# The first expert block's products with down_embed as stages of each group's mlp during the scan, kept in DRAM

## Chip, cores and metric

One core of a Trainium2 chip runs the whole kernel as one program. The metric is the device time of one execution in microseconds; less is better.

## What is computed

x has 4 x 1024 tokens of width 256, all in f32. Four layers follow one another, each added to x after a layer norm (ln):

```python
x = x + attn_a(ln(x))   # state-space block: projections, a convolution of 4 taps, a scan with 16 states per channel
x = x + ffn(ln(x))      # first expert block
x = x + attn_b(ln(x))   # linear attention, 16 heads
x = x + ffn(ln(x))      # second expert block
```

The change is in the first `ffn`. With h = ln(x), per token:

```python
queries = (h @ W_q).reshape(2, n, 64); routing = einsum('tnd,tdk->tnk', queries, keys)
# the 8 best of each half, and the 8 best of their 64 sums, choose the experts and give `scores`
ew = silu(einsum('nh,nkh->nk', h, down_embed[indices])) * softmax(scores)
experts = einsum('nk,nkh->nh', ew, up_embed[indices])
mlp = (silu(h @ gate_w) * (h @ up_w)) @ down_w
ffn = mlp + experts
```

There are 512 experts. The kernel doesn't gather their rows: it multiplies h with all 512 rows of down_embed, takes silu, and multiplies with a table that is zero but for the chosen experts.

## The kernel before, in words

The 4096 tokens are worked on in 8 groups of 512 (`G`); two groups are one sequence of the batch. A tile with features on the 128 partitions and a group's 512 tokens along the row is 128x512; 512 experts are four such pieces (`XC`), the mlp's 1024 inner channels eight (`IC`).

**The scan.** `ssm` (line 142) runs 8 groups x 16 states = 128 steps, each in two half steps (`half`, 256 in all). A half step has, on ACT, two decays `a` (`decay`, 908); on POOL, one product `u` (`times_b`, 889), made three half steps ahead; on DVE, two scans `h<-a,u`; then, for the step before (`sum_up`, 919), eight transposes `hT` on PE and two accumulations `acc` on DVE. In this text half steps are numbered from 0 to 255, so that group g begins with half step 32 g.

**What runs beside the scan.** After the scan's own instructions of a half step, `tick` (681) adds stages of other work. A stage is the code between two `yield`s of a generator, and the `yield` states its cost on PE and on ACT. There are three queues: `prep` (`prepare`, 333: the next group's projections, convolution and step sizes), `ends` (`finish`, 495, and `norm`, 544: the end of the group before, its layer norm and the transposed `hT`, stored to the DRAM tensor `hs`) and `mlps` (`mlp`, 574). `tick` takes stages as far as budgets allow, 3.2 us of PE time and 2.7 of ACT time a half step. Everything here is recorded through `Pinned` (37), so each engine runs these instructions in the order in which the code emits them, and all of them carry line 47 in the profile.

**The mlp of a group** has 8 gate stages (two matmuls, 128x512, and one stage later ACT's copy into `av`), one silu over `av`, 8 up stages, and 8 down stages (two for each of 4 token tiles). A product with up is multiplied into `av` either by ACT's copy (`up_v`) and POOL, or by DVE from PSUM; `room` decides (580). Each token tile of the down product is added to x by DVE (`xw<-xw,down`). The weights are streamed in pieces of 128 KB through three buffers (`ask_w`, 534), 8 of gate_w, then 8 of up_w, for each group. At the end x is stored to the DRAM tensor `xs`, and `load_x(g + 4)` (640) asks for the tile of x that reuses its buffer.

At the 27th half step of group g (line 978) the sums over x of group g + 2 begin:

```python
if q % (2 * N) >= 26 and g + 2 < NG and g + 2 not in counted:
    while g + 2 not in xw:
        mlps.stage()
    counted.add(g + 2)
    stats = statistics(g + 2)
```

`statistics` (241) begins with four ACT instructions (`junk<-xw`) that read that tile of x.

**The block.** `experts` (1505) follows the scan. For each group it runs 8 steps. `route` (1309) finds the best experts on DVE and builds the table `tb` on ACT (`entries`) and POOL. `apply` (1553) makes four products `emb` of `hT` with down_embed (two matmuls each), four silus into `wt`, multiplies `wt` by the transposed table (`st` on PE, `weigh` on DVE), and makes the products `o` with up_embed, which DVE adds to x. `hT` is loaded from `hs`. `beside` (1631) takes further stages from `ends` and `mlps`, by a table `COST` of each step's own PE time, until both are empty; then, from group 4 on, `attention_pools` loads the attention's weights, and `attend` runs stages of `first_batch` (1057), the layer norms, keys and queries of the first sequence. At the start of a group's steps, the code first runs all stages that its x still needs (`while g not in rest.stored`).

`attention` (1125) and `ffn` (1734) come last and aren't touched.

Of the kernel before, what the change touches and what calls it, by code (L numbers as in the profile page):

```python
# [12 lines left out]
F32 = mybir.dt.float32  # L13
I16, BF16 = mybir.dt.int16, mybir.dt.bfloat16
AF = mybir.ActivationFunctionType
# [5 lines left out]
P = 128  # L21
B, L, D = 4, 1024, 256
NT = B * L
KD = D // P
G = 512
NG = NT // G
# [25 lines left out]
class Net:  # L52
# [86 lines left out]
        return ps  # L139


    def ssm(self, xs, hs, behind):


        nc, tc, io = self.nc, self.tc, self.io
# [3 lines left out]
        with ExitStack() as ctx:  # L149
# [18 lines left out]

            xw, gates, norms, bcds, sums, first = {}, {}, {}, {}, {}, {}
            ended, gated_all, stored = {-2, -1}, {-2, -1}, set()  # L170

            def load_x(g):
                xw[g] = late4.tile([P, TG, D], F32, tag="x", name="xw")
# [356 lines left out]
                ended.add(g)  # L530

            ahead_w, asked_w = [], [0]

            def ask_w():
                i = asked_w[0]
                if i < NG * 2 * IC:
                    name = "gate_w" if i // IC % 2 == 0 else "up_w"
                    w = late3.tile([P, KD, P], F32, tag="gu", name=name)
                    src = io[name].rearrange("(k p) (c m) -> c p k m", p=P, m=P)
                    sp.dma_start(out=w, in_=src[i % IC])  # L540
                    ahead_w.append(w)
                    asked_w[0] += 1

# [30 lines left out]
            def mlp(g, hT):  # L574
# [437 lines left out]
            for half in range(2):  # L1012
# [2 lines left out]
            scan.close()  # L1015
            behind(
                SimpleNamespace(
                    engines=engines, ends=ends, mlps=mlps, bank=bank, stored=stored,
                    route0=route0, first_h=first_h, key_w=key_w, lates=lates,
                )  # L1020
            )
# [480 lines left out]
                self.x[g][:, t, :], self.x[g][:, t, :], ps, ALU.add  # L1502
            )

    def experts(self, w, xpool, xs, hs, rest):


        tc, nc, ends, mlps, bank = self.tc, rest.engines, rest.ends, rest.mlps, rest.bank
        with ExitStack() as ctx:
# [16 lines left out]
            asks, hT, routes, tables = dict(rest.first_h), {}, {}, {}  # L1526
            self.x, self.total = {}, {}

            half = NG // 2

            def load(into, g):
                while g == NG - 1 and ends.next_cost():
                    ends.stage()
                tag = "hT" if into is hT else f"ask{g // half}"
                into[g] = two.tile([P, KD, G], F32, tag=tag, name=tag)
                nc.sync.dma_start(out=into[g], in_=hs[g])

            def product(ps, pairs):
                for i, (lhsT, rhs) in enumerate(pairs):
# [12 lines left out]

            def apply(g):

                h = hT.pop(g)
                wt = two.tile([P, XC, G], F32, tag="wt", name="wt")

                def emb(c):
                    ps = bank([P, G], "emb")
                    cs = slice(c * P, (c + 1) * P)  # L1560
                    product(ps, [(w["down_embT"][:, k, cs], h[:, k, :]) for k in range(KD)])
                    return ps
# [7 lines left out]
                yield  # L1570
                ps = emb(1)
                yield
                silu(1, ps)
                yield
                yield
                for c in (2, 3):
                    if c == 3:
                        silu(2, ps)
                    ps = emb(c)
                    yield  # L1580
                silu(3, ps)
# [74 lines left out]
            next(routes[0])  # L1656
            next(routes[0])
            beside(1.7)
            load(hT, 0)
            applied = []  # L1660
            for step in range(8 * NG + 7):
                g, k = step // 8, step % 8
                if k == 0 and g < NG:
                    while g not in rest.stored:
                        ends.stage()
                        mlps.stage()
                    self.x[g] = xpool.tile([P, TG, D], F32, tag=f"x{g}", name=f"x{g}")
                    self.total[g] = xpool.tile([P, TG], F32, tag=f"sum{g}", name=f"sum{g}")
                    nc.sync.dma_start(out=self.x[g], in_=xs[g])
                if k == 1 and g < NG:  # L1670
                    applied.append(apply(g))
                for a in list(applied):
                    if next(a, self) is self:
# [3 lines left out]
                if g + 1 < NG:  # L1677
# [3 lines left out]
                        next(routes[g + 1])  # L1681

                    if k == 5 and g % 2 == 0 and g + 2 < NG:
                        load(asks, (g + 2) // 2)
                        load(asks, (g + 2) // 2 + half)
# [80 lines left out]
def build(nc, io, out):  # L1766
    with tile.TileContext(nc) as tc, ExitStack() as ctx:
        net = Net(ctx, tc, io)
        kept = ctx.enter_context(tc.tile_pool(name="kept", bufs=1, space=DRAM))
        xs = [kept.tile([P, TG, D], F32, tag=f"xs{g}", name=f"xs{g}") for g in range(NG)]  # L1770
        hs = [kept.tile([P, KD, G], F32, tag=f"hs{g}", name=f"hs{g}") for g in range(NG)]
        w = net.expert_weights(ctx.enter_context(tc.tile_pool(name="ex_w", bufs=1)))

        def behind(rest):
            xpool = ctx.enter_context(tc.tile_pool(name="x", bufs=1, reuse_waits="tile"))
            net.experts(w, xpool, xs, hs, rest)

        net.at_ctx = ExitStack()
        net.ssm(xs, hs, behind)
# [55 lines left out]
```

## Time and profile before

| | us |
|---|---|
| median of 3 runs (1937.09 to 1939.22) | 1938.54 |
| the profiled execution | 1938.45 |
| its span, first to last instruction | 1936.7 |
| PE busy, of the span | 1767.3 (91%) |
| DVE busy | 1487.1 (77%) |
| ACT busy | 1178.7 (61%) |
| POOL busy | 996.9 (51%) |
| last scan of DVE ends at | 1033.4 |
| 32 products `emb` (128 matmul records) | 60.6 |
| 32 silus `wt<-emb` | 19.0 |

PE is TensorE's matmuls, PEld its weight loads, DVE VectorE, ACT ScalarE, POOL GpSimd, SP the engine that issues most DMAs. One f32 matmul of the program is two records in the profile. Times in the views are microseconds from the span's start, unless marked ns. A row of the timeline has start, time taken, engine, line, operation, output and inputs by the program's names, shapes, count, and in brackets the idle time before it and what ended it. The profile's share for an engine is an average over the scan (to 1033 us), the block (to some 1295 us) and the two last layers.

### The profile page before, as it was taken

What the parts mean: (1) busy time and instruction counts of PE and PEld (TensorE: products, weight loads), DVE (VectorE), ACT (ScalarE), POOL (GpSimd) and SP (SyncE); (2) the same over time, 40 slices, a digit from 0 to 9 for tenths busy, and PEclk for the clock granted to TensorE, in tenths of its full rate; (3) what the DMA queues carried; (4) which work ended last, traced back from release to release, by engine and by line L of the source; (5) the groups of instructions that cost most, each with busy time, mean ns of one, the idle gap of its engine ahead of it and who ended that gap; (6) DMA issues with size and microseconds to landing.
All of it is one profiled execution on the core that took longest, in us unless ns stands there. A gap on an engine that the chain in (4) does not pass through costs nothing.

```text
span 1936.7 us, 22863 instructions
## 1 busy us (share of the span) xinstructions
PE 1767.3 (91%) x7450; PEld 1138.9 (59%) x7450; DVE 1487.1 (77%) x2653; ACT 1178.7 (61%) x2335; POOL 996.9 (51%) x810
## 2 busy tenths in 40 slices
PE   7867789989889898898978999899999999999999
PEld 4445446556456465565645757566666566655665
DVE  6999999999999999999999979734549544433441
ACT  5876798787987878878555664744434333323330
POOL 4978989899988988888862122221111000000000
PEclk8868899999999999999999999999999999999999
DMA  4212121221322212212133121120000000000000
GB/s 127 65 34 60 40 88 54 82 72 57 94 64 73 79 47 82 79 47 77 50 101 127 61 63 68 61 65 1 1 1 1 11 11 12 0 12 11 11 12 11
DMA packets 79928, 97.48 MB, mean 50 GB/s; under 512 B 7360, under 2 KB 53312, under 8 KB 79808
## 3 DMA queue, kind: packets, MB, share of 16 engines
q1 hardware_dynamic: 74592, 90.66, 14.8%
q10 hardware_dynamic: 5216, 5.36, 0.9%
q8 instruction: 59, 0.97, 0.2%
q14 instruction: 61, 0.50, 0.1%
HBM read 83.15 MB, written 12.85 MB: 50 GB/s over the span
## 4 chain that ended last, share of the span: by engine, by line
PE 40%; DVE 9%; ACT 4%; issue 1%; POOL 0%; DVEq 0%; ACTq 0%; POOLq 0%
PE ps L136 23%; PE o L47 3%; PE emb L47 2%; PE down L47 2%; PE at L47 1%; PE up L47 1%; DVE acc L47 1%; PE gate L47 1%; DVE kept L1392 1%; PE st L1470 1%; DVE h L47 1%; PE tr L127 1%; PE route L1304 1%; PE hT L47 1%; ACT a L47 1%
## 5 line engine op out<-in xcount | busy, mean ns | idle before, releaser
L47 POOL TENSOR_TENSOR u<-dx,bt 128x1024 f32<-128x1024 f32 x255 | 601.9, 2363 | 79.6 <-DVE h L47 66.0
L47 DVE TENSOR_TENSOR_SCAN h<-a,u 128x512 f32<-128x512 f32 x512 | 608.1, 1226 | 16.5 <-ACT a L47 14.2
L47 PE MATMUL hT<-ident,h 128*128 128x128 f32 x2048 | 310.8, 292 | 104.0 <-DVE acc L47 103.7
L47 ACT ACTIVATE a<-delta,a_neg 128x512 f32<-128x512 f32 x512 | 340.1, 688 | 96.8 <-DVE h L47 96.0
L47 PEld LDWEIGHTS hT<-ident,h 128*128 128x128 f32 x2048 | 246.1, 149 | 240.9 <-DVE acc L47 195.8
L47 DVE SCALAR_TENSOR_TENSOR acc<-hT,cT,acc 128x512 f32<-128x512 f32 x512 | 353.9, 731 | 12.4 <-PE hT L47 11.4
L1460 POOL TENSOR_TENSOR tb<-tb,kept 128x1024 f32<-128x1024 f32 x16 | 34.0, 2130 | 364.7 <-DVE kept L1453 364.7
L1731 DVE TENSOR_TENSOR act<-s,ps 128x512 f32<-128x512 f32 x64 | 43.9, 686 | 146.3 <-PE ps L136 145.5
L47 PE MATMUL up<-hT,up_w 128*128 128x512 f32 x256 | 131.2, 637 | 11.0 <-ACT up_v L47 10.8
L1729 ACT ACTIVATE s<-ps 128x512 f32<-128x512 f32 x64 | 38.2, 597 | 168.4 <-PE ps L136 168.3
L47 PE MATMUL gate<-hT,gate_w 128*128 128x512 f32 x256 | 122.1, 600 | 0.0
L136 PE MATMUL ps<-hT,w_gate_w 128*128 128x512 f32 x256 | 120.6, 592 | 0.0
L136 PE MATMUL ps<-hT,w_up_w 128*128 128x512 f32 x256 | 120.5, 592 | 0.0
L136 PE MATMUL ps<-w_down_w,act 128*128 128x256 f32 x512 | 117.5, 380 | 1.9 <-DVE x L1501 1.9
L47 POOL TENSOR_TENSOR xc<-xc,tap 128x512 f32<-128x512 f32 x84 | 109.1, 1299 | 18.8 <-ACT tap L47 18.6
L47 PE MATMUL down<-w_down_w,av 128*128 128x256 f32 x512 | 118.1, 379 | 0.0
L136 PEld LDWEIGHTS ps<-w_down_w,act 128*128 128x128 f32 x512 | 95.7, 190 | 20.3 <-DVE x L1501 7.7
L47 ACT ACT_TABLE_LOAD x77 | 98.8, 1283 | 13.8 <-DMA w_wd2T<-in_wd2T 8.9
L47 PEld LDWEIGHTS down<-w_down_w,av 128*128 128x128 f32 x512 | 94.9, 190 | 16.7 <-issue 5.5
L47 POOL TENSOR_TENSOR tb<-tb,kept 128x1024 f32<-128x1024 f32 x16 | 34.8, 2175 | 126.3 <-DVE kept L47 44.3
L1384 ACT ACTIVATE tb<-d,ex 128x64 f32<-128x64 f32 x256 | 62.1, 334 | 45.0 <-DVE ex L1375 42.0
L47 PEld LDWEIGHTS up<-hT,up_w 128*128 128x128 f32 x256 | 47.8, 202 | 61.3 <-issue 40.4
(301 smaller groups left out, 3089.3 us busy)
## 6 DMA issues: line engine op xcount, KB each, us to landing
bt<-bcd SPq DMA_DIRECT2D x127, 256.0 KB, 3.3
gate_w<-in_gate_w SPq DMA_DIRECT2D x64, 128.0 KB, 2.3
up_w<-in_up_w SPq DMA_DIRECT2D x64, 128.0 KB, 2.3
in_wT<-in_in_wT SPq DMA_DIRECT2D x8, 512.0 KB, 4.8
hs<-hT SPq DMA_DIRECT2D x8, 512.0 KB, 2.9
xs<-xw SPq DMA_DIRECT2D x8, 512.0 KB, 2.7
hT<-hs SPq DMA_DIRECT2D x8, 512.0 KB, 5.2
x<-xs SPq DMA_DIRECT2D x8, 512.0 KB, 4.6
```

The costliest lines, as they stand in the source:

```text
L47: return self.tc.keep_in_program_order(f(*args, **kw))
L127: self.nc.tensor.transpose(ps[:, t * P : (t + 1) * P], src[:, t, k * P : (k + 1) * P], self.ident)
L136: self.nc.tensor.matmul(ps, lhsT=lhsT, rhs=rhs, start=i == 0, stop=i == len(pairs) - 1)
L1304: nc.tensor.matmul(ps[:, t, m, :], lhsT=h[:, k, col], rhs=w["scores"][t][:, k, :], start=k == 0, stop=k == KD - 1,)
L1384: nc.scalar.activation(tbv[:, m, i, :], d[:, M4 + m, 0:NKEY], AF.Copy, scale=ex[:, m, i : i + 1],)
L1392: dve.tensor_tensor(kept, v[:, M4:, :].unsqueeze(3).to_broadcast(shk), r[:, M4:, :].unsqueeze(2).to_broadcast(shk), ALU.is_gt,)
L1460: nc.gpsimd.tensor_tensor(tbv[:, ms], tbv[:, ms], kept[:, ms], ALU.mult)
L1470: self.nc.tensor.transpose(st[:, c, :], tb[:, i, c * P : (c + 1) * P], self.ident)
L1729: nc.scalar.activation(s, pg, AF.Silu)
L1731: nc.vector.tensor_tensor(a, s, pu, ALU.mult)
```

## The change

The four products of h with down_embed leave `apply` and become four stages of `mlp`, between the gate stages and the silu. Their weights are streamed as 4 further pieces of 128 KB a group. Each product is copied by ACT to an SBUF tile (`emb_v`, of the same two buffers as `up_v`) and stored to a new DRAM tensor `es[g]`. In the block, `load_wt` loads the 128x2048 tile of a group from `es`, and `apply` begins with one silu over it. `hT` is no longer loaded there. `apply` starts six steps later than before, so that its steps after the silu stand where they stood; the loads of x move by as much. `COST` and the budget of `beside` are changed (3.3 a step instead of 3.5).

```diff
+            shelved = set()
...
             ahead_w, asked_w = [], [0]
+            stream = [
+                (name, c)
+                for name, n in (("gate_w", IC), ("down_embT", XC), ("up_w", IC))
+                for c in range(n)
+            ]
...
-                if i < NG * 2 * IC:
-                    name = "gate_w" if i // IC % 2 == 0 else "up_w"
+                if i < NG * len(stream):
+                    name, c = stream[i % len(stream)]
...
-                    sp.dma_start(out=w, in_=src[i % IC])
+                    sp.dma_start(out=w, in_=src[c])
...
                 act.copy(av[:, IC - 1, :], ps)
+
+                def shelve(c, ps):
+                    t = late2.tile([P, G], F32, tag="up", name="emb_v")
+                    act.copy(t, ps)
+                    sp.dma_start(out=es[g][:, c, :], in_=t)
+
+                for c in range(XC):
+                    yield 1.7, (0.6 if c else 0)
+                    if c:
+                        shelve(c - 1, ps)
+                    ps = bank([P, G], "emb")
+                    w = ahead_w.pop(0)
+                    mul(ps, [(w[:, k, :], hT[:, k, :]) for k in range(KD)])
+                    ask_w()
+                yield 0, 0.6
+                shelve(XC - 1, ps)
+                shelved.add(g)
                 yield 0, 6.4
                 act.activation(av, av, AF.Silu)
...
+            def load_wt(g):
+                while g not in rest.shelved:
+                    ends.stage()
+                    mlps.stage()
+                wts[g] = two.tile([P, XC, G], F32, tag="wt", name="wt")
+                nc.sync.dma_start(out=wts[g], in_=es[g])
...
             def apply(g):
 
-                h = hT.pop(g)
-                wt = two.tile([P, XC, G], F32, tag="wt", name="wt")
-
-                def emb(c):
...
-                def silu(c, ps):
-                    nc.scalar.activation(wt[:, c, :], ps, AF.Silu)
-
-                ps = emb(0)
+                wt = wts.pop(g)
+                nc.scalar.activation(wt, wt, AF.Silu)
                 yield
-                silu(0, ps)
...
-            COST = (0.9, 1.7, 0.9, 1.7, 3.4, 4.3, 1.7, 1.7)
+            COST = (0.9, 0, 0.9, 0, 3.4, 5.1, 0, 0)
 
             def beside(cost):
-                left[0] = min(left[0] + 3.5, 6.0) - cost
+                left[0] = min(left[0] + 3.3, 6.0) - cost
...
-                if k == 0 and g < NG:
+                if k == 6 and g < NG:
                     while g not in rest.stored:
                         ends.stage()
                         mlps.stage()
...
-                if k == 1 and g < NG:
+                if k == 7 and g < NG:
                     applied.append(apply(g))
...
-                    if k == 6:
-                        load(hT, g + 1)
+                if k == 4 and g < NG:
+                    load_wt(g)
...
+        es = [kept.tile([P, XC, G], F32, tag=f"es{g}", name=f"es{g}") for g in range(NG)]
```

More of the change, by code (lines that the diff above doesn't have):

```diff
@@ L139, in product, with ssm @@
         return ps
-    def ssm(self, xs, hs, behind):
+    def ssm(self, xs, hs, es, behind):
         nc, tc, io = self.nc, self.tc, self.io
@@ L1017, in ssm @@
                 SimpleNamespace(
-                    engines=engines, ends=ends, mlps=mlps, bank=bank, stored=stored,
+                    engines=engines, ends=ends, mlps=mlps, bank=bank, stored=stored, shelved=shelved,
                     route0=route0, first_h=first_h, key_w=key_w, lates=lates,
@@ L1503, in raise_x, with experts @@
             )
[L1505 removed]
+    def experts(self, w, xpool, xs, hs, es, rest):
         tc, nc, ends, mlps, bank = self.tc, rest.engines, rest.ends, rest.mlps, rest.bank
@@ L1525, in experts, with load_ask @@
                 w["scores"][t] = key_w[:, t, :, :]
-            asks, hT, routes, tables = dict(rest.first_h), {}, {}, {}
+            asks, wts, routes, tables = dict(rest.first_h), {}, {}, {}
             self.x, self.total = {}, {}
             half = NG // 2
-            def load(into, g):
+            def load_ask(g):
                 while g == NG - 1 and ends.next_cost():
                     ends.stage()
-                tag = "hT" if into is hT else f"ask{g // half}"
-                into[g] = two.tile([P, KD, G], F32, tag=tag, name=tag)
-                nc.sync.dma_start(out=into[g], in_=hs[g])
+                tag = f"ask{g // half}"
+                asks[g] = two.tile([P, KD, G], F32, tag=tag, name=tag)
+                nc.sync.dma_start(out=asks[g], in_=hs[g])
+            def load_wt(g):
[4 more added lines that the diff above has]
+                nc.sync.dma_start(out=wts[g], in_=es[g])
             def product(ps, pairs):
@@ L1553, in apply @@
             def apply(g):
-                h = hT.pop(g)
-                wt = two.tile([P, XC, G], F32, tag="wt", name="wt")
-                def emb(c):
[L1559 to L1562, printed above, removed]
-                def silu(c, ps):
-                    nc.scalar.activation(wt[:, c, :], ps, AF.Silu)
-                ps = emb(0)
-                yield
-                silu(0, ps)
[L1570 to L1581, printed above, removed]
+                wt = wts.pop(g)
+                nc.scalar.activation(wt, wt, AF.Silu)
+                yield
                 tb = tables.pop(g)[0]
@@ L1658, in experts @@
             beside(1.7)
-            load(hT, 0)
             applied = []
@@ L1683, in experts @@
                     if k == 5 and g % 2 == 0 and g + 2 < NG:
-                        load(asks, (g + 2) // 2)
-                        load(asks, (g + 2) // 2 + half)
-                    if k == 6:
-                        load(hT, g + 1)
+                        load_ask((g + 2) // 2)
+                        load_ask((g + 2) // 2 + half)
+                if k == 4 and g < NG:
+                    load_wt(g)
                 if not early and g >= FROM and ends.next_cost() is None is mlps.next_cost():
@@ L1775, in behind @@
             xpool = ctx.enter_context(tc.tile_pool(name="x", bufs=1, reuse_waits="tile"))
-            net.experts(w, xpool, xs, hs, rest)
+            net.experts(w, xpool, xs, hs, es, rest)
         net.at_ctx = ExitStack()
-        net.ssm(xs, hs, behind)
+        net.ssm(xs, hs, es, behind)
         net.mlp_weights(
```

## The prediction

> **What bounds the kernel now.** I read the busy time by stage first, then the timeline of single engines inside the scan, then the groups by line. Columns of the first view: stretch, length, then busy time (and count) of PE, PEld, DVE, ACT, POOL, then granted clock, DMA share, GB/s.
>
> ```profile
> core 0: us, PE busy (x) PEld busy (x) DVE busy (x) ACT busy (x) POOL busy (x), PEclk, DMA share, GB/s
> 250.00:1033.00 783.00, 693.45 (x3192) 443.56 (x3191) 758.64 (x905) 619.55 (x1043) 677.97 (x519) 0.97 0.23 70
> 1039.40:1230.10 190.70, 183.79 (x768) 126.05 (x766) 165.43 (x500) 113.73 (x321) 39.19 (x40) 1.00 0.24 82
> 1230.10:1295.00 64.90, 59.48 (x240) 39.89 (x241) 26.86 (x85) 36.19 (x102) 10.60 (x11) 0.97 0.15 49
> ```
>
> Row one is the scan: DVE is busy 758.6 of 783 us, PE 693.5. Row two is the expert block, from the first routing maximum of group 0 to that of group 7: there PE leads (183.8 of 190.7), with DVE close behind (165.4). Row three runs to the first `po` product of the attention. So the work to be moved leaves a PE stage for a DVE stage.
>
> How a half step of the scan is filled decides the cost of moving. DVE, then PE, around 850 us:
>
> ```profile
> 843.83 1.38 DVE L47 SCALAR_TENSOR_TENSOR acc<-hT,cT,acc 128x512 f32<-128x512 f32 x2
> 845.13 2.33 DVE L47 TENSOR_TENSOR_SCAN h<-a,u 128x512 f32<-128x512 f32 x2
> ...
> 849.08 2.33 DVE L47 TENSOR_TENSOR_SCAN h<-a,u 128x512 f32<-128x512 f32 x2
> 851.32 1.38 DVE L47 SCALAR_TENSOR_TENSOR acc<-hT,cT,acc 128x512 f32<-128x512 f32 x2
> 853.07 0.42 DVE L47 TENSOR_TENSOR xw<-xw,down 128x256 f32<-128x256 f32 x1 [0.36 <-PE down L47]
> 853.40 2.33 DVE L47 TENSOR_TENSOR_SCAN h<-a,u 128x512 f32<-128x512 f32 x2
> ```
> ```profile
> 850.26 1.04 PE L47 MATMUL hT<-ident,h 128*128 128x128 f32 x8
> 851.13 3.62 PE L47 MATMUL down<-w_down_w,av 128*128 128x256 f32 x16
> 854.59 1.04 PE L47 MATMUL hT<-ident,h 128*128 128x128 f32 x8
> ```
>
> A half step is two scans and two accumulations: 3.5 us from scan to scan at best (841.58 to 845.13). Here it is 4.3 (849.08 to 853.40), because PE's eight transposes and two down stages take 4.3. One 1.72 us product fits under 3.5 us, two do not.
>
> ACT, around half step 154 (its scans start at 634.08), and two rows of the DMA issues (KB, us to landing):
>
> ```profile
> 632.28 1.30 ACT L47 ACTIVATE a<-delta,a_neg 128x512 f32<-128x512 f32 x2
> ...
> 633.61 0.42 ACT L47 ACTIVATE junk<-xw 128x256 f32<-128x256 f32 x1
> ...
> 635.21 0.71 ACT L47 ACTIVATE xc<-xc,w_W_D 128x512 f32<-128x512 f32 x1
> 635.83 0.57 ACT L47 COPY av<-gate 128x512 f32<-128x512 f32 x1
> 636.29 1.31 ACT L47 ACTIVATE a<-delta,a_neg 128x512 f32<-128x512 f32 x2
> ```
> ```profile
> xs<-xw SPq DMA_DIRECT2D x8, 512.0 KB, 2.7
> xw<-in_x SPq DMA_DIRECT2D x7, 512.0 KB, 3.9
> ```
>
> ACT reads the next x tile (`junk<-xw`, four times, about 0.5 apart) between the decays `a` of one half step and those of the next. If that tile has not landed, the decays wait behind it, and DVE's scans wait for the decays.
>
> **The change, part by part.** In the built program's order 24 of the 32 products run inside the scan. The queue pushes out 3 gate and 5 up products in exchange, so PE in the scan gains 16 products net: 16 x 1.72 = 27.5 us, and PE behind the scan loses 27.5.
>
> 1. DVE in the scan. Because of the shifted stages 19 products with up are multiplied by DVE instead of 10 (`av<-up,av`, 0.68 us each): 9 x 0.68 = **+6.1**. POOL loses 9 x 1.27 = 11.4, worth nothing, since DVE ends the half steps.
>
> 2. PE in the scan. Cost between 0 (all in PE's 89.6 idle us) and +27.5 (all on the path). I took each half step's PE sum and DVE sum from the rows and let PE run 0.5 us late before DVE pays. That gives 120.1, five times 125.5 and 119.4 for groups 1 to 7; the trace has 120.9, 125.5, 126.3, 125.4, 129.6, 126.9, 119.0. In the new order the same sums, without point 3, come out about **+5**. An empty half step takes a product for nothing, a half step with a `skip` product does not.
>
> 3. x tiles. Line 979 runs stages of the mlp until x of group g+2 is asked for, at half step 26 of group g. Four more stages per mlp make it late. At half step 154 the new order drains two down tiles at once, at half step 186 three. The load waits for the store of the old x in its buffer, and that for the last down add. Half step 154: transposes 1.04 and four down stages of 1.73, 8.0; add 0.4; store 2.7; load 3.9; four sums 2.0; `xc` 0.7; decay 0.7: 18.4 instead of the 4.7 that DVE itself needs, +13.7. Half step 186: 11.4 of PE, so 21.8 instead of 5.1, +16.7. In group 3 the last down add ends half step 120, the load lands 6.6 later, and half step 122 waits about 3. Together **+33.4**; with the load hidden only PE's drain stays, 3.3 + 6.3 = +9.6, the lower end. Queued behind the waiting sums on ACT: `xc`, then every decay.
>
> 4. In the scan, at nothing: 24 ACT copies of 0.58 (14 us, less 12 up copies and 5 gate copies that leave; ACT idles 163 us of 783), weight loads of 128 KB and stores of 256 KB on SP (DMA share 0.23). SP waits for these copies, but would wait longer for the weight buffer behind. If that cover went, ACT's net is 14 - 9.9 = +4.1.
>
> 5. The block up to group 7. PE loses its lead and DVE takes over. DVE's 165.4, less 11 multiplications and 8 down adds (7.5 + 3.4) that leave this stretch, plus 8 and 4 that come (5.4 + 1.7), is 161.6. The two intervals in which DVE came nearest to filling (21.9 of 22.8, 25.4 of 27.2) had 1.3 us of waits each; seven such, 170.7: **-20**. Ends: -29 (DVE without a wait) and 0. The wt load (1 MB; 8.7 for the slowest load of that size) is asked three steps ahead of its silu, some 10 us, and one silu of 1.91 replaces four of 0.6 off the path. Were it late for each group, up to 8 x 8.7.
>
> 6. The end of the block. Now the first attention batch starts beside group 6, before the routing of group 7, and both fill PE. In the new order the drain of group 7's mlp stands inside group 7's routing on DVE, and the batch's layer norms stand behind that routing on POOL. From group 7's maximum: DVE to its sixth multiplication 20.4; eight down stages 13.8 and an add 0.4; two raises and the second `kept` 2.2; POOL's table 5.6; first layer norm 6.0; table load and silu on ACT 3.2; second layer norm 5.8; transposes and copy 1.5. That is 58.9. Then PE: eight rows of keys and gates at 3.03 (two 0.86, 0.86, 0.45), `qT` 6.9, `o` 6.9. Sum 96.9 against 64.9: **+32**. Lower end: PE's own sum in this stretch, 74.5, +9.6. Upper: +36, with mask building on POOL not hidden.
>
> Sum: 6.1 + 5 + 33.4 - 20 + 32 = +56.5. The profiled execution took 1938.45 us (span 1936.7 and 1.75 around it), the median of three is 1938.54. **Forecast 1995.**
>
> **A rule against this.** PE looks full in the scan by matmul time, 693 of 783. The Trainium skill, "Perfetto Trace Analysis", section "Identifying the Most-Contended Engine", says that matmul busy time is no good measure of PE's headroom and that the weight loads' busy share is. By PEld, 444 of 783, point 2 would be 0. The trace speaks against this use of it: the half steps above have PE, not DVE, at their end.
>
> **Rivals.**
>
> A. One of the two long waits is hidden: the loads of point 3 land in time (-23.8), or the last batch is held by PE alone (-22.4). About 1972. For it: ACT runs up to half a step ahead. Against it: both are chains of single instructions in one order.
>
> B. Both hidden: 1995 - 46.2 = 1949.
>
> C. Faster. PE's room in the scan takes the products (points 2 and 3 cost nothing), and the block, bound by PE as now, gives back all 27.5: 1938.45 + 6.1 - 27.5 = 1917. It decides if the last down add comes two half steps (7 us, over 2.7 + 3.9) ahead of half steps 154 and 186, and if DVE's waits in the block vanish. For it: 89.6 idle us on PE. Against it: DVE at 165 of 191.
>
> D. The change does little: the pushed-out gates and ups refill the block, and the scan has room. 1938, within 0.2% (3.9 us, about what a measurement of this kernel can tell from no change).
>
> **How the numbers follow.** Forecast 0.50, A 0.25, B 0.10, C 0.08, D 0.03, beyond 2020 0.04. The range 1950 to 2020 leaves out C, D, the part beyond, and half of B: 0.20. Its ends take in point 3 at 9.6 with point 6 at its lower end, and upward the block without gain. Faster is C, 0.08; same is D and 0.02 of B, 0.05; slower 0.87.
>
> **What would show it.** Scan: group 4 and 5 longer by 14 to 17 us each, with one gap on DVE, ended by ACT `a`, at half steps 154 and 186, and ACT waiting for the DMA `xw<-in_x`. Otherwise group 2 and 3 by 4 to 9. Block: intervals between routing maxima of 21 to 27 us with DVE over 90% busy; PE idle for 20 us after the last down stage, waiting for ACT `ln`. It is wrong if ACT never waits for `xw`, or if PE stays over 95% busy in the block.

## The result and the profile after

The changed kernel takes 2025.49 us (median, 2025.30 to 2026.47), the kernel before 1938.88 beside it: a ratio of 1.0449, 95% interval 1.0437 to 1.0461, or 86.6 us slower. The forecast was 1995, the range ended at 2020: direction and places were right, the size was too small by 30 us. Spans by stage, from the two profiled executions:

| stretch, us | before | after | difference | forecast |
|---|---|---|---|---|
| start to first scan | 38.6 | 35.8 | -2.8 | 0 |
| first to last scan | 994.8 | 1056.6 | +61.8 | +44.5 |
| last scan to the maximum of group 0 | 6.0 | 5.3 | -0.7 | 0 |
| to the maximum of group 7 | 190.7 | 173.4 | -17.3 | -20 |
| to the first `po` | 64.7 | 109.6 | +44.9 | +32 |
| from there to the end | 641.9 | 643.1 | +1.2 | 0 |

The first scan begins between 35.5 and 38.9 us in the 18 profiles of this study, with nothing changed ahead of it; that row is scatter. The same three stretches after the change (columns as in the prediction: busy time and count of PE, PEld, DVE, ACT, POOL, granted clock, DMA share, GB/s):

```profile
250.00:1092.00 842.00, 729.57 (x3248) 455.26 (x3248) 769.05 (x911) 615.36 (x1045) 658.48 (x504) 0.96 0.25 75
1097.70:1271.10 173.40, 150.13 (x635) 105.41 (x634) 159.94 (x492) 114.47 (x296) 37.77 (x31) 0.95 0.36 123
1271.10:1380.70 109.60, 86.07 (x316) 57.13 (x315) 34.23 (x100) 42.47 (x117) 15.53 (x21) 0.86 0.19 64
```

The scan is longer by 59 us, yet DVE's busy time grew by only 10: the rest is waiting. In the block PE's share fell from 96% to 87% and DVE's rose from 87% to 92%, as forecast. The last stretch holds 34 us of DVE and 86 of PE in 110: a chain.

What DVE waited for in the scan, after the change (us, times, longest):

```profile
DVE h L47 <- ACT a L47: 48.1, 25, 9.6
DVE xw L47 <- PE down L47: 12.2, 9, 3.0
DVE acc L47 <- PE hT L47: 8.8, 16, 1.3
```

Before, the first of these rows was:

```profile
DVE h L47 <- ACT a L47: 10.9, 14, 1.3
```

Two of the waits for the decays `a` after the change, 9.4 and 9.6 us, are the gaps at half steps 154 and 186. Without them 29.1 us are left, still 18.2 more than before. ACT after the change has a row that was not there before:

```profile
ACT junk L47 <- DMA xw<-in_x: 38.5, 4, 19.8
```

Half step 154, all engines (PEld, POOL and the accumulator reads left out):

```profile
653.56 2.34 DVE L47 TENSOR_TENSOR_SCAN h<-a,u 128x512 f32<-128x512 f32 x2 [2.41 <-ACT a L47]
...
653.98 7.07 PE L47 MATMUL down<-w_down_w,av 128*128 128x256 f32 x32
...
661.09 0.42 DVE L47 TENSOR_TENSOR xw<-xw,down 128x256 f32<-128x256 f32 x1 [3.03 <-PE down L47]
...
661.54 0.32 SPq L47 DMA_DIRECT2D xs<-xw  x1
...
664.16 0.38 SPq L47 DMA_DIRECT2D xw<-in_x  x1
...
667.90 0.42 ACT L47 ACTIVATE junk<-xw 128x256 f32<-128x256 f32 x1 [13.71 <-DMA xw<-in_x]
...
670.13 1.28 ACT L47 ACTIVATE a<-delta,a_neg 128x512 f32<-128x512 f32 x2
670.90 1.22 DVE L47 TENSOR_TENSOR_SCAN h<-a,u 128x512 f32<-128x512 f32 x1 [9.38 <-ACT a L47]
```

The chain of point 3 stands here link by link: four down stages on PE, the add, the store (2.6 us until the load begins), the load (3.7), the sums, `xc`, the decay, and only then DVE. From scan to scan 17.3 us.

Behind the maximum of group 7, at 1271.11, PE and ACT:

```profile
1292.74 6.00 PE L47 MATMUL o<-w_up_emb,wt 128*128 128x256 f32 x16 [4.49 <-DVE x L47]
1298.58 13.98 PE L47 MATMUL down<-w_down_w,av 128*128 128x256 f32 x64
...
1337.22 5.87 PE L47 MATMUL o<-w_up_emb,wt 128*128 128x256 f32 x16
1342.93 1.88 PE L47 MATMUL at<-wkv,hT 128*128 128x512 f32 x4
```
```profile
1320.95 0.51 ACT L47 ACTIVATE ln<-x,sum 128x256 f32<-128x256 f32 x1 [30.93 <-POOL sum L47]
```

The last mlp is drained here, 14 us of PE, and the first layer norm of the attention waits behind it and behind POOL; the first `at` comes 71.8 us after the maximum.

### The profile page after: what moved, and what is told of

Read it like the earlier page. It is cut to its first block, busy times and chain, and to the rows that moved or that the text cites. A ratio compares the mean times of both kernels' runs of the same rounds, so it can differ in the third digit from the quotient of the medians.

```text
span 2023.7 us, 23002 instructions
## 1 busy us (share of the span) xinstructions
PE 1798.3 (89%) x7450; PEld 1148.8 (57%) x7450; DVE 1501.6 (74%) x2665; ACT 1184.3 (59%) x2329; POOL 982.6 (49%) x798
## 4 chain that ended last, share of the span: by engine, by line
PE 47%; DVE 27%; ACT 15%; issue 7%; POOL 2%; DMA 1%; DVEq 0%; SPq 0%; POOLq 0%; ACTq 0%
PE ps L136 22%; DVE h L47 7%; DVE acc L47 6%; PE hT L47 4%; PE down L47 4%; ACT a L47 4%; ACT L47 2%; DVE kept L47 2%; PE gate L47 2%; ACT xc L47 1%; PE dt L47 1%; PE up L47 1%; PE xin L47 1%; PE at L47 1%; PE bc L47 1%
## 5 line engine op out<-in xcount | busy, mean ns | idle before, releaser
L47 DVE TENSOR_TENSOR_SCAN h<-a,u 128x512 f32<-128x512 f32 x512 | 615.1, 1240 | 55.8 <-ACT a L47 51.7
L47 PE MATMUL hT<-ident,h 128*128 128x128 f32 x2048 | 316.5, 294 | 123.6 <-DVE acc L47 122.4
L47 ACT ACTIVATE a<-delta,a_neg 128x512 f32<-128x512 f32 x512 | 339.4, 688 | 99.9 <-DVE h L47 98.8
L47 PE MATMUL gate<-hT,gate_w 128*128 128x512 f32 x256 | 126.7, 621 | 0.7 <-ACT av L47 0.7
L136 PEld LDWEIGHTS ps<-hT,w_up_w 128*128 128x128 f32 x256 | 48.5, 190 | 57.7 <-issue 56.4
```

The source lines that it names most:

```text
L47: return self.tc.keep_in_program_order(f(*args, **kw))
L136: self.nc.tensor.matmul(ps, lhsT=lhsT, rhs=rhs, start=i == 0, stop=i == len(pairs) - 1)
```

## Experiments

"The groups" are the eight sums of 32 half steps, from first scan to last: 992.4 us before, 1054.3 after.

**1. Are the x tiles the loss in the scan?** In the first kernel the product stages, and their place in the weight stream, move behind the down stages:

```diff
-                for name, n in (("gate_w", IC), ("down_embT", XC), ("up_w", IC))
+                for name, n in (("gate_w", IC), ("up_w", IC), ("down_embT", XC))
...
                 if g + 4 < NG:
                     load_x(g + 4)
+                for c in range(XC): ...  # shelve and product, as before the silu
```

> The changed kernel with the four product stages moved behind the mlp's down stages, the store of x and the load of the next x (the weight stream in the same order: gate, up, down_embT). Nothing is left out. Theory W (the x tiles are late because four stages stand ahead of the down stages): half steps 154 and 186, 17.3 and 21.4 us in the changed kernel, fall back to 4 to 7 us, ACT's wait for the load of x (38.5 us) falls under 10, and the time falls by 25 to 33, to 1992 to 2000. Theory R (PE is short of room for 16 more products, and the two drains only collect that debt in two places): the gaps go, but other half steps grow by as much; groups 4 and 5 together stay over 285 us (292.0 now, 255.0 before), and the time falls by less than 10.

Measured: 1987.99 us, ratio 1.0258 (1.0243 to 1.0274). Half steps 154 and 186 take 3.5 and 6.6, ACT's wait for x is 4.8. The two gaps are all but gone, 28.6 us less; but the groups still sum to 1028.7, 36.3 of the 61.9 us that the change had added, and groups 4 and 5 to 271. Theory W holds for the two gaps; over half of the loss in the scan is something else. The time fell by 37.5, more than the 33 expected, since the last stretch fell too, by 10.8.

In the second the drain stays and only ACT's sums come later:

```diff
-                        counted.add(g + 2)
-                        stats = statistics(g + 2)
+                        if q % (2 * N) >= 29:
+                            counted.add(g + 2)
+                            stats = statistics(g + 2)
```

> The changed kernel, where ACT's sums over the next x tile are begun three half steps later (half step 29 of a group instead of 26); the drain of the mlp at half step 26 stays as it is. Nothing is left out. Theory W: the gap at half steps 154 and 186 is PE's drain first, then ACT waiting for the load with the decays behind it; later sums take away the second part, DVE's two waits of 9.4 and 9.6 us for the decays: 18 to 20 us less, about 2007, with half steps 154 and 186 at 8 and 12 us. Rival (the drain alone, PE's four and six stages in one half step, is what DVE waits for, and the load would be hidden): less than 5 us, over 2020.

Measured: 2014.07, ratio 1.0393 (1.0376 to 1.0410), 11.4 less, between the two expectations. Half steps 154 and 186 fell to 7.9 and 11.7, 19.1 less as expected, but others grew by 8 in sum. The load wait and PE's drain are two parts of each gap, some 9.5 us of load in each.

**2. What would the block gain at most?**

```diff
-                for c in range(XC): ...   # product, copy, store
+                sp.dma_start(out=es[g], in_=av[:, :XC, :])
```

> The changed kernel without the 32 products at all: neither in the scan nor in the block; what the block loads in their place is a copy of a part of av, so the output isn't the reference's. It shows what the block alone gains when 32 products of 1.72 us leave it. Theory V (without the products DVE bounds the block): the scan takes as long as in the kernel before (994.8 us, +-5), the intervals between the maxima sum to 165 to 175 us (190.7 before), and the time is 1905 to 1935, so that the move could never have given more than 35 of the 55 us of PE time. Rival C (PE's time comes straight off): 1938 - 55 = 1883, intervals at 140 to 150.

Measured: 1918.73, ratio 0.9903 (0.9888 to 0.9918). The groups sum to 997.9, the intervals to 180.1, the last stretch takes 53.5. With all 55 us of products gone the kernel gains 19. Theory V holds in the time; the intervals are 5 us longer than it had, and the scan, 1000.3 us, is 0.5 over its bound. DVE, not PE, is next:

```profile
1041.50:1221.60 180.10, 150.16 (x664) 112.83 (x662) 164.99 (x501) 110.94 (x305) 42.59 (x41) 0.92 0.32 115
```

DVE's 165.0 here stand beside 165.4 before: its work didn't change, and it is now the fuller engine. The 19 us are the ceiling of this block, with its one silu a group (experiment 4), and not of every way to move the products.

**3. The end of the block.**

```diff
-                left[0] = min(left[0] + 3.3, 6.0) - cost
-                for q in (ends, mlps):
+                left[0] = min(left[0] + 5.0, 7.5) - cost
+                for q in (ends, mlps, mlps):
```

> The changed kernel, where the block runs up to two mlp stages beside each of its own steps (allowance 5.0 a step and 7.5 at most, instead of 3.3 and 6.0). Nothing is left out. Theory S (the end of the block is long since the mlp of group 7 is drained late, behind it the first attention batch): the mlp is done some groups earlier, the batch starts beside earlier groups, and the stretch from the last routing maximum to the first po product falls from 109.6 to 65 to 80 us: 1985 to 2000. Rival (this stretch is as long as PE's and ACT's own work in it, whatever the order): what is drained earlier makes the intervals between the maxima longer by as much, 2020 to 2030.

Measured: 2003.96, ratio 1.0339 (1.0324 to 1.0355), 21.5 less than the changed kernel. Neither expectation holds as it stands. The last stretch fell by far more than expected, from 109.6 to nothing, but the intervals sum to 221.1 instead of 173.4 and what follows `po` takes 682.1 instead of 643.1. The late drain costs, though by this edit only 21 us of the 110 can be had.

> The kernel before, with up to two mlp stages beside each of the block's steps (allowance 5.0 and 7.5 instead of 3.5 and 6.0). Nothing is left out. Theory (in the kernel before PE is full in the block, 183.8 of 190.7 us, so what is drained earlier only changes places): 1938 within 6 us, the intervals between the maxima longer by as much as the stretch from the last maximum to po is shorter. Rival (the gain of 21 us that the same edit made in the changed kernel has nothing to do with the change): 1915 to 1925.

The same two lines (from 3.5) in the kernel before: 1955.75, ratio 1.0085 (1.0070 to 1.0101). Intervals 233.4 (+42.7), last stretch 30.8 (-33.9), behind it +8.4. Both expectations missed: two stages a step are a loss of 18 us here. The intervals grow by nearly as much as in the changed kernel (42.7 and 47.7); what differs is the end, where the last stretch and what follows `po` fall by 25.5 together here, and by 70.9 there. So the 21 us gained in the changed kernel come out of the last stretch that the change had lengthened, not out of room in the intervals.

> The changed kernel with both edits: the product stages behind the mlp's down stages, and up to two mlp stages beside each step of the block. Nothing is left out. Theory (late x tiles in the scan and the late drain at the block's end are two separate losses): the gains add, 37.5 + 21.5 = 59 us from the changed kernel's 2025.5, about 1966 (1962 to 1972); that it is still slower than before (1938) is the price of PE's 24 products in the scan. Rival (the end of the block is helped by the first edit alone, since it also moves the mlps' drain): 1980 to 1988.

Measured: 1976.92, ratio 1.0196 (1.0179 to 1.0213), 48.6 less than the changed kernel instead of 59, between the two expectations. Moving the stages had already cut the last stretch by 10.8 (109.6 to 98.8), which the sum of the two gains counts twice. Two separate losses, with one overlap.

**4. One silu by itself.** In the kernel before:

```diff
-                    nc.scalar.activation(wt[:, c, :], ps, AF.Silu)
+                    nc.scalar.copy(wt[:, c, :], ps)
...
+                nc.scalar.activation(wt, wt, AF.Silu)
```

> The kernel before, where the block's four silus of a product (0.6 us each) become four ACT copies, and one silu over 128x2048 follows them, as in the changed kernel; the products stay in the block. Nothing is left out. Theory (ACT is busy 113.7 of 190.7 us in the block and is not what bounds it, so the one silu a group is worth nothing by itself): 1936 to 1941. Rival (the four silus cost table loads or waits on the path, and the one silu saves them): 1925 to 1933, and part of the block's shorter intervals in the changed kernel is due to it.

Measured: 1950.38, ratio 1.0058 (1.0043 to 1.0073): 12 us slower, which neither expected. The intervals sum to 196.5 (+5.8), the last stretch takes 71.3 (+6.6); DVE's waits for ACT's `wt` in the block rise from 1.4 us to 11.2. Four short silus beside the products are cheaper here than four copies and one silu behind them. In the changed kernel the one silu stands ahead of the steps that need it and has no copies beside it; that place wasn't tested by itself, and nothing here shows the silu to be a source of the gain in the block.

**5. PE's time, ACT's copies, or the stages' places?** 30 to 36 us stay in the scan of e1_behind_down. First its matmuls alone are taken out, then the copies too:

```diff
-                    act.copy(t, ps)
+                    act.copy(t, av[:, c, :])
...
-                    ps = bank([P, G], "emb")
-                    w = ahead_w.pop(0)
-                    mul(ps, [(w[:, k, :], hT[:, k, :]) for k in range(KD)])
+                    ahead_w.pop(0)
```

> The kernel e1_behind_down in the same order of stages, with the 32 products' matmuls left out: their four stages a group still stand in the queue with the same cost, their weights are still loaded, and ACT copies and SP stores a piece of av in place of the product, so the output isn't the reference's. What differs in the scan is PE's 24 x 1.72 = 41 us. In e1_behind_down the eight groups of half steps sum to 1028.6 us, in e4_left_out (no stages at all) to 997.8. Theory P (PE's idle time in the scan is the tail of half steps that end on DVE, so that a moved product costs nearly its own time): at least two thirds of the 30.8 us go, the groups sum to 998 to 1008, and the time is 1957 to 1969. Rival L (the copies, stores and loads, DVE's ten more multiplications and the shifted places of ACT's long silus cost it): the groups stay over 1018, the time over 1977.

Measured: 1984.80, ratio 1.0236 (1.0221 to 1.0251); the groups sum to 1024.4. Without 41 us of matmuls the scan is shorter by 4.3. Theory P, that PE's idle time can't be used, falls. The matmuls that stay ran at a lower granted clock (0.90 over the scan, 0.93 in e1_behind_down), so the products' own price may be somewhat over 4.3.

> The kernel e7_no_matmul (e1_behind_down's order of stages, no product matmuls) without ACT's copies either: the four stages a group only take their budget, load their weights, and SP stores a piece of hT to the place of the product, so the output isn't the reference's. In e7_no_matmul the groups of half steps sum to 1024.3 us, in e4_left_out to 997.8; of that difference the matmuls' share has been taken away already. Theory Q (the stages' places in the queue): the groups stay over 1018, the time over 1974. Theory K (ACT's 32 copies, at the 1.4 us each that 12 of them cost in e12_two_free against e14_no_copies): the groups fall to 998 to 1006, the time to 1955 to 1966. Half each would be 1010 to 1015.

Measured: 1971.30, ratio 1.0184 (1.0167 to 1.0202), the groups at 1023.1. The copies of this order cost 1.3. The 30.7 us above the kernel before come with no product and no copy at all; 6.8 of them are ten more multiplications `av<-up,av` on DVE, and the rest is mostly this row (here from 250 us on):

```profile
DVE h L47 <- ACT a L47: 28.8, 20, 3.7
```

Over the whole scan DVE's waits for `a` are 14.2 us before, 32.7 in e1_behind_down, 32.8 in e7_no_matmul and 32.4 here: neither the matmuls nor the copies, nor the lower clock, move them.

The cross test puts four stages without any instruction into the kernel before:

```diff
+                for _ in range(4):
+                    yield 1.7, 0.6
                 yield 0, 6.4
                 act.activation(av, av, AF.Silu)
```

> The kernel before, with four empty stages in each group's mlp ahead of its silu: they take the queue's budget (1.7 us of PE, 0.6 of ACT each) and emit no instruction. Nothing is left out. Theory Q: with nothing added to any engine the scan gets longer nearly as in the changed kernel (half steps 154 and 186 above 12 us, the groups 50 us or more over the 992.4 of before), and with the stages pushed into a block that PE bounds the time is 1990 to 2020. Rival (work makes time: instructions that are not there cost nothing): within 10 us of 1938.

Measured: 2029.97, ratio 1.0477 (1.0462 to 1.0493), above the range of Theory Q and somewhat slower than the changed kernel itself, with no instruction in the stages and no load or store for them. (Six more products with up are multiplied by DVE instead of POOL, 4.1 us, as their places shift.) Half steps 122, 154 and 186 take 17.7, 21.2 and 21.4; the groups sum to 1061.0. Outside these three half steps that is 19 us more than before, 15 without the six multiplications. DVE and ACT, empty stages:

```profile
DVE h L47 <- ACT a L47: 48.8, 21, 9.7
DVE xw L47 <- PE down L47: 17.6, 10, 3.0
```
```profile
ACT junk L47 <- DMA xw<-in_x: 54.0, 4, 19.8
```

These are the rows of the changed kernel, with a longer wait for x. In the kernel before, the half steps repeat with a period of 32: an mlp just fills one. The silus of `av` begin in half steps 64, 97, 128, 161, 192, 224 and 251, at most one later than a whole period. In the changed kernel they begin in 68, 104, 141, 174, 206 and 238: each mlp starts later in its period than the last, by some four half steps a group, until x of group g + 2 is due and the drain stops the drift. That the silu and the adds land beside other long instructions on the way is the likely reason for the rest of the loss; no run takes these meetings apart.

**6. The products outside the queue.** If places cost and products don't, products at chosen half steps must be nearly free. The queue holds no product of groups 0 to 5; they are emitted at fixed half steps:

```diff
+            AT = {31: 0, 9: 1, 12: 2, 17: 3}
...
+                    while placed and placed[0][0] < q:
+                        shelve(*placed.pop(0)[1])
+                    if q % (2 * N) in AT:
+                        c = AT[q % (2 * N)]
+                        ge = g - 1 if c == 0 else g - 2
+                        if 0 <= ge < NG - 2:
+                            placed.append((q, emb(ge, c)))
```

> The changed kernel, where the products of groups 0 to 5 are no stages of the queue: each is emitted at a fixed half step of the scan (31, 9, 12 and 17 of each 32), two of which hold no mlp stage and two a single one, beside what the queue put there, so that the order of everything else is that of the scan without products (groups 6 and 7: stages behind the down stages). ACT's copy follows a half step later. Nothing is left out. Theory Q (a stage in the queue costs its place, not its PE time: four more stages a group push the mlp's other stages into half steps that are already full on DVE or ACT, and that is what e1_behind_down and e7_no_matmul both paid, 31 us against e4_left_out): with 24 products in the scan its groups still sum to 992 to 1006 us, and the time is 1925 to 1945. Rival (the products' own PE time, or ACT's copies and the stores, cost it wherever they stand): the groups sum to 1015 or more, the time is over 1950.

Measured: 1968.17, ratio 1.0149 (1.0132 to 1.0166), the groups at 1028.5. Theory Q missed, and both numbers are the rival's. The longest half steps are numbers 10 and 11 of their 32, 7.3 to 7.7 us, and ACT shows why:

```profile
ACT emb_v L50 <- POOL av L50: 30.8, 5, 6.8
```

The copy waits for a buffer that POOL still reads (`up_v` shares it), and the decays wait behind the copy. Other half steps:

> The kernel e9_placed with other fixed half steps: 31, 17, 20 and 22 of each 32 instead of 31, 9, 12 and 17. In e9_placed ACT waited 30.8 us, 5 times, with its copy of a product for POOL's multiplication by up: both use the two buffers named up, and half steps 9 and 12 lie in the up stages. Half steps 22 and 31 hold no mlp stage, 17 a single one, 20 a z product and four transposes. Nothing is left out. Theory Q, mended (24 products outside the queue cost only what PE lacks in their half step: nothing at 22 and 31, some 0.6 at 17 and 1.0 to 1.4 at 20, and ACT no longer waits for a buffer): the groups of half steps sum to 998 to 1010 us (992.4 before, 1028.4 in e9_placed), the time is 1935 to 1952. Rival (24 products cost 30 us in the scan wherever they stand): the groups sum to 1020 or more, the time is over 1958.

Measured: 1951.29, ratio 1.0075 (1.0061 to 1.0088), the groups at 1013.9, between both expectations (the time is within Theory Q's); that wait is gone. Then only the two products of each group that fall in half steps without an mlp stage, the other two staying in the block (`AT = {31: 0, 22: 1}`, 12 products):

> The kernel before with only two of the four products of groups 0 to 5 moved, 12 in all, each to a half step of the scan that holds no mlp stage (31 and 22 of each 32), outside the queue; the block loads these two pieces of a group and makes the other two products as before (groups 6 and 7 as before). Nothing is left out. Theory Q: the scan's groups sum to 990 to 999 us (992.4 before), and the block, 12 products or 20.6 us of PE shorter, gives back the 19.2 x 12/32 = 7 us that e4_left_out gave for all 32, or somewhat more: 1928 to 1937. Rival (the block gains nothing, since the load of the moved pieces and the silu over them come late, or the scan pays): 1940 to 1955.

Measured: 1942.82, ratio 1.0025 (1.0016 to 1.0035), the groups at 1007.5: 15 us for 12 products, against Theory Q. ACT at half step 130:

```profile
536.58 3.62 ACT L50 ACTIVATE av<-av 128x4096 f32<-128x4096 f32 x1
540.10 0.57 ACT L50 COPY emb_v<-emb 128x512 f32<-128x512 f32 x1
540.57 0.59 ACT L50 COPY up_v<-up 128x512 f32<-128x512 f32 x1
541.18 1.28 ACT L50 ACT_TABLE_LOAD   x1
542.47 0.69 ACT L50 ACTIVATE a<-delta,a_neg 128x512 f32<-128x512 f32 x1
```

The copy of the product stands behind the longest instruction of ACT and ahead of the decay that DVE waits for. It also keeps its PSUM buffer, one of three that these products share, until it has run, and PE waits for that:

```profile
PE yT L50 <- ACT emb_v L50: 15.6, 5, 3.5
```
```profile
540.72 1.11 PE L50 MATMUL yT<-ident,acc 128*128 128x128 f32 x4 [2.88 <-ACT emb_v L50]
546.14 1.57 DVE L50 SCALAR_TENSOR_TENSOR acc<-hT,cT,acc 128x512 f32<-128x512 f32 x2 [1.72 <-PE hT L50]
```

Behind this wait PE's next `up` takes 3.62 us instead of 1.88 (granted clock 0.52 from 540.72 to 547.00), and the transposes that DVE's `acc` needs come late. In the kernel before, PE waits at the same place 1.9 us for an `up_v` of ACT, behind these `yT`, and its `up` takes 1.98. Two tests of the copy:

```diff
-                t = late2.tile([P, G], F32, tag="up", name="emb_v")
-                act.copy(t, ps)
-                sp.dma_start(out=es[g][:, c, :], in_=t)
+                sp.dma_start(out=es[g][:, c, :], in_=hTs[g][:, c, :])
```

> The kernel e12_two_free (products at half steps 31 and 22) without ACT's 12 copies: SP stores a piece of hT in place of the product, so the output isn't the reference's; the products themselves are still made. Theory K: the copies are the price, the groups of half steps sum to 992 to 999, the time is 1928 to 1936. Rival (the price is PE's, the product of half step 31 in front of the transposes of the next ones): over 1003, the time over 1938.

Measured: 1931.05, ratio 0.9959 (0.9943 to 0.9974), the groups at 990.6. Theory K holds: 12 products cost nothing here, their 12 copies on ACT 16.9 us, 1.4 each for an instruction of 0.57. PE's wait for `emb_v` is gone; 13.4 us of waits for `up_v` take its place (10.8 before).

> The kernel e12_two_free with its first product moved from half step 31 to half step 17 of each 32, one period of 32 later for the same group; the second stays at 22. Nothing is left out. In e12_two_free the groups of half steps sum to 1007.4 us (992.4 before), and of the ten half steps that differ from before by over 0.9 us six are number 2 of their 32, where ACT's silu of 128x4096 lies between two table loads and the copy of the product from half step 31 (0.57 us) lies behind it, before the decays. Theory K (a copy on ACT isn't free next to that silu): without a copy there the groups sum to 992 to 1000, the time is 1930 to 1937. Rival (12 products cost 15 us in the scan wherever they stand): the groups stay over 1004, the time over 1940.

Measured (`AT = {17: 0, 22: 1}`): 1939.04, ratio 1.0002 (0.9994 to 1.0011), no difference from before; the groups at 1003.3, between both expectations. PE's wait for `emb_v` is gone here too, yet away from the silu the 12 products with their copies still cost 11 us, so the silu is only part of it; no run at these half steps leaves the copies out. The other engine:

```diff
-                act.copy(t, ps)
+                dve.tensor_copy(t, ps)
```

> The kernel e12_two_free with DVE making the 12 copies of a product instead of ACT. Nothing is left out. Theory K (ACT's copies were the price; DVE ends the half steps, so a copy of some 0.6 us costs its own time there, and nothing where DVE waits for ACT's silu): the groups of half steps sum to 990.6 + 3.5 to 7.5 = 994 to 998 us, the time is 1930 to 1938. Rival (any engine that has to take the product out of PSUM next to the silu delays PE's banks, and the price stays): the groups stay over 1003, the time over 1939.

Measured: 1926.11, ratio 0.9946 (0.9934 to 0.9959): the version that beats both kernels, with everything computed, by 11 us. The groups sum to 991.5, below Theory K's range and 0.9 above e14_no_copies, although DVE makes 12 copies of 0.68 (8.2 us). DVE in e12_two_free, then with its own copies:

```profile
DVE h L50 <- ACT a L50: 15.9, 16, 2.2
DVE acc L50 <- PE hT L50: 11.4, 19, 1.7
DVE xw L50 <- PE down L50: 6.9, 19, 0.4
```
```profile
DVE h L50 <- ACT a L50: 10.8, 15, 1.1
DVE xw L50 <- PE down L50: 5.0, 14, 0.4
DVE acc L50 <- PE hT L50: 3.6, 6, 0.9
```

Its waits fall by 14.8, of the 16.0 between the two kernels' groups: 5.1 in those for the decays, but 7.8 in those for PE's transposes. So the copy on ACT was dear by two ways, and by these rows the longer one led over PE. The block gives 3.6 in the intervals and 4.9 in the last stretch.

## Why the prediction fell short

Of the 30 us missing, some 16 belong to point 2, 13 to point 6 and 3 to point 5; the rest is small.

1. **DVE in the scan, +6.1.** Right: 19 multiplications by DVE in the profile; 12.9 us against 6.8. (POOL lost 13, not 9.)
2. **PE in the scan, +5.** The size of PE's own part was about right, 4.3 in e7_no_matmul; the step that failed is the list of what else is late. "I took each half step's PE sum and DVE sum from the rows and let PE run 0.5 us late": ACT wasn't in it, though it feeds every scan. The scan's +61.8 less 34.4 for half steps 122, 154 and 186 leaves 27.4, where points 1 and 2 had 11.1. The missing 16 are displaced stages that make ACT's decays late: DVE's waits for `a`, without those of half steps 122, 154 and 186 (2.5, 9.4 and 9.6), are 15.7 longer in the profile after, and e16_no_copies (24) and e10_empty_stages (15) show such a loss with no product in the stages. The rule weighed there (the Trainium skill, "Perfetto Trace Analysis", "Identifying the Most-Contended Engine"), read by the weight loads' share alone, would have made this point 0. The 4.3 us measured lie nearer to the forecast's 5, yet most of the matmuls' 41 us was free, as the rule has it. The rule says nothing on places.
3. **x tiles, +33.4.** Right: 17.3, 21.4 and 6.2 at half steps 154, 186 and 122, +34.4; the forecast had 18.4 and 21.8. Its four sums at 2.0 were too long (in its own rows they stand 0.4 apart, 1.6 in all), which is part of the difference at 154. What it took for two incidents is the end of a drift of some four half steps a group.
4. **At nothing.** True in the queue's order (1.3 us for the copies in e16_no_copies), but not in general: 12 copies cost 17 us in e12_two_free, part of it by a way that wasn't on the list, PE's wait for the buffer that the copy has to empty.
5. **Block, -20.** Right in kind: -17.3, DVE at 92%. The last interval came out at 23.8 after 31.2. PE's idle time after the last down stage is there too, but 15.7 us in four gaps up to the first `at` instead of 20, and only 7.5 of it behind ACT's `ln`.
6. **End of the block, +32.** Right in kind, +44.9. Of the 12.9 missing, 7.2 lie ahead of the down stages (they end 41.4 us after the maximum, not 34.2, since the second half of an `o`, which the sum left out there, stands ahead of them on PE: it waits 4.5 for DVE to empty one of two buffers and then takes 6.0 where 3.6 is usual), and 5.7 behind them, where another half `o` of 5.87 runs ahead of the first `at`. From `at` to `po` it took 37.8, forecast 38; that is in part luck, since only half of the 6.9 us of `o` fell there and the eight rows took 2.6 more.

Rival C, 21 us faster, failed in the scan, which didn't take the products for nothing: points 2 and 3 and the displaced stages cost over 50 us. Where the products are gone altogether, in e4_left_out, the gain is 19, near C's sum, but for all 32 products and not for 16 net: DVE bounds the block next, as argued against C.

Still open: which collisions make up the 24 us of displaced stages in e16_no_copies one by one, why the products and copies of e13_two_later cost 11 us away from the silu, how the price of a copy in e12_two_free divides between the decays and PE's wait, and whether a product at 17 or 20 would also be free with DVE's copy, which wasn't tried.

## What to carry to other kernels

Where a hand-made queue fills a periodic loop exactly, a new stage costs its place before it costs its work: put the same number of empty stages into the kernel before, and the run prices the displacement roughly, apart from the instructions. Price a moved step on the in-order engine that feeds the bounding one, not only on the engine that does the work, and ask which buffer it holds meanwhile: a 0.6 us copy on ACT cost 1.4 us, and under 0.1 on the engine that was waiting for ACT and PE. And ask what the emptied stage is bound by next: leaving the work out (e4_left_out) gives the ceiling of that arrangement in one run.

## What the runs showed of the hardware

PE's matmuls of equal shape get longer after a pause, and the granted clock is lower over them: the 16 `o` matmuls at 1284.64 take 3.62 us, one every 0.22, at a clock of 1.00. The 16 behind a wait of 4.5 take 6.00, at 0.61: the first ten start 0.43 or more apart, the last five 0.22 again, and the 64 of `down` behind them run at 1.00. The 16 at 1337.22, amid waits, take 5.87, at 0.61 too.

In the scan, taking matmuls out lowered the granted clock: 0.953 to 0.958 over the whole run in the four runs of e1_behind_down, 0.936 or 0.937 in those of e7_no_matmul. PE's busy time over the scan falls by less than the work that left: from 892.7 to 859.6 us, 33 of 41.
